# Attention's matmuls as 64x64 tiles, four at a time, in a two-layer convolution kernel

## The chip, the cores and the metric

One core of a Trainium2 chip runs the whole program. The metric is device time in microseconds (us), the median of several runs. PE is TensorE, PEld its weight loads, DVE VectorE, ACT ScalarE, POOL GpSimd, SP SyncE, which here issues nearly all DMAs. PSUM is the memory that PE writes; it is used here in banks of 512 columns of 32 bits.

## What is computed

Two blocks over 8 images of 512 channels and 1024 pixels (tokens), all in 32-bit floats. The first is group norm, q, k, v, attention with 8 heads of 64 channels, a projection, a group norm and the residual. The second is attention with one head of 512 channels over weight-normed projections. Only the first block's attention is touched by the change. Cut to what matters:

```python
hn = group_norm(x, gn1_scale, gn1_bias)
qkv = jnp.einsum('bchw,oc->bohw', hn, w_qkv) + b_qkv[None, :, None, None]
qkv = qkv.reshape(b * NHEAD, 3 * ch, n)
q, k, v = jnp.split(qkv, 3, axis=1)
wgt = jnp.einsum('bct,bcs->bts', q * scale, k * scale)
wgt = jax.nn.softmax(wgt, axis=-1)
a = jnp.einsum('bts,bcs->bct', wgt, v).reshape(b, c, h, w)
out = jnp.einsum('bchw,oc->bohw', a, w_proj) + b_proj[None, :, None, None]
x = x + group_norm(out, gn2_scale, gn2_bias)
# then the second block, on x
```

## The kernel before

**Tiles on PE.** Each 32-bit matmul appears as two records, each with its own weight load; each record streams all columns of the moving operand. A label such as 64\*128 gives the rows and columns of PE's array that a matmul takes: 128\*128 is all of it, 64\*128 one half of the rows (two such matmuls can run side by side on `halves[0]` and `halves[1]`, each into a bank of its own), and 128\*64 one half of the columns (two side by side, into the two halves of one bank's partitions).

**The steps.** An image's attention is 32 steps (`STEPS`, line 370): four pairs of heads `j`, eight blocks `r` of 128 tokens each. `Heads.step` (line 636) issues, for step `i`:

- `softmax(i)`: on DVE two reductions (`nm<-s`, one per head), on ACT two exponentials (`p<-s,nm`).
- in every second step from step 5 on (`LAG`, line 370) `values(g)` (line 611): 16 matmuls of 256 columns into one bank, then one evacuation on ACT (`a<-po`), which frees the slot of `pT`.
- `fill`: in the steps between, one piece of the next pair's q and k. In images 1 to 7 it also holds the last products of the layer before: a 128\*128 one in step 0, and `products_rows` (line 1105, 64\*128) in steps 1 and 2.
- `scores(i + 1)` (line 559): four 64\*128 matmuls of 512 columns into two double banks (tag `sc`, three of them).
- `turn()` (line 586): DVE's transpose (`pb<-p`) of the step before and its four DMAs into `pT`.
- `scale()` (line 604): a reciprocal on DVE, and on POOL two multiplications of `p`.
- `later`: POOL's additions that complete q and k, and other work.

Each engine takes its instructions in the order in which the program issues them (`InOrder`, line 26).

**The pieces of q and k.** `project_rows` (line 398) splits each product by rows: two 64\*128 chains into two banks, evacuated by ACT and added by POOL. It serves image 0, and the first pair of the next image. `project_seven` (line 476), for the other three pairs of images 1 to 7, has four pieces: piece 0 is two whole 128\*128 matmuls of 512 columns; pieces 1, 2 and 3 are eight 64\*128 matmuls each. After piece 0, in the steps 8 and 16, a quarter of the next values is done ahead (lines 1299 to 1301). The steps of image 1 and later in which pieces are projected are set at line 1288.

**Banks.** `bank()` (line 114) takes from two PSUM banks in turn (tag `mm`). The pieces of q and k take both, the values one.

Of the kernel before, what the change touches and what calls it, by code (L numbers as in the profile page):

```python
# [10 lines left out]
AF = mybir.ActivationFunctionType  # L11
# [41 lines left out]
def attention_blocks_kernel(  # L53
# [318 lines left out]

    def project_qk(b, j, hn):
# [24 lines left out]
    def project_rows(b, j, hn, spare):  # L398
# [6 lines left out]
        def pieces():  # L405
            for t in (1, 0):
# [3 lines left out]
                for th in range(2):  # L410
                    hs = slice(th * HN, (th + 1) * HN)
                    pms = [bank(f"pqk_{b}_{j}_{t}_{th}_{r}") for r in range(2)]
                    for ci in range(CI):
                        for r in range(2):
                            PE.matmul(
                                pms[r],
                                w[halves[r], ci, :],
                                hn[halves[r], ci, hs],
                                start=(ci == 0),
                                stop=(ci == CI - 1),  # L420
                            )
# [54 lines left out]
    def project_seven(b, j, right):  # L476
# [13 lines left out]
        def add(to, a, b_):  # L490
            return lambda: PO.tensor_add(to, a, b_)

        adds = (
            ([], []),
            ([], []),
            ([add(q2, q2, q1), add(k2, k2, turned(q2))], [add(k1, k1, k2), add(k2, k2, turned(tmp[1]))]),
            ([add(q1, q1, tmp[0]), add(q2, q2, tmp[1])], [add(q2, q2, tmp[2])]),
        )

        def pieces():  # L500
            pm = bank(f"pq7_{b}_{j}_0")
            run(matmuls(pm, [(w[:, k, :], right(None, 0, k)) for k in range(2)]))
            AC.copy(tmp[1], pm)
            yield adds[0]
            for n in range(1, 4):
                pms = [bank(f"pq7_{b}_{j}_{n}_{r}") for r in range(2)]
                for k in range(CI):
                    for r in range(2):
                        PE.matmul(pms[r], w[halves[r], CI * n - 2 + k, :], right(r, n, k), start=(k == 0), stop=(k == CI - 1))
                if n == 1:  # L510
                    AC.activation(q1, pms[0], AF.Identity, bias=bqs[:, j : j + 1])
                    AC.copy(k1, turned(pms[1]))
                elif n == 2:
# [39 lines left out]
    class Heads:  # L553
        def __init__(self, b, hn, v, qk):
            self.b, self.hn, self.v, self.a = b, hn, v, None
            self.qk = {0: qk}
            self.pT, self.ps, self.waiting, self.open = {}, None, None, None

        def scores(self, i):
# [3 lines left out]
            for c in range(2):  # L563
                cs = slice(c * HN, (c + 1) * HN)
                for hh in range(2):
                    PE.matmul(
                        self.ps[hh][:, cs],
                        qk[halves[hh], 0, r * P : (r + 1) * P],
                        qk[halves[hh], 1, cs],
                        start=True,  # L570
# [924 lines left out]
```

## Time and profile before

| | |
|---|---|
| runs, median of 3 | 3202.4 us (3199.84 to 3202.9) |
| profiled execution, span from first to last instruction | 3197.2 us |
| scores (`s<-qk`), records x mean | 2048 x 603 ns |
| values (`po<-pT,v`), records x mean | 4096 x 382 ns |
| q and k of `project_seven` (`pq`, 64\*128) | 1008 records, mean 589 ns |
| piece 0 of `project_seven` (`pq`, 128\*128) | 84 records, mean 610 ns |
| q and k of `project_rows` (`pqk`, 64\*128) | 640 records, mean 590 ns |
| granted TensorE clock, mean | 0.998 |

The page of the profile gives each engine's busy time, and the chain of work that ended last, followed back from the last instruction. A timeline lists instructions in order of time: start in us, how long, the engine, what it writes and reads (out<-in), the rows\*columns of the array and the shape, how many records were merged (x8), and in brackets how long the engine was idle before it and what ended that. Records of matmuls overlap: a record of 512 columns lasts some 590 ns while the next starts 429 ns after it.

### The profile page before, as it was taken

The page shows a single profiled execution, that of the slowest core. Times are in us where ns is not written, and L with a number is a line of the kernel's source. Part 1 is how long each engine was busy: PE and PEld are TensorE (multiplying, and loading weights), DVE is VectorE, ACT ScalarE, POOL GpSimd, SP SyncE. Part 2 cuts the span into 40 slices and gives each one's busy share as a digit, 9 for nine tenths or more (in the row PEclk, how much of TensorE's full clock was granted, in tenths as well). Part 3 has the DMA queues.
Part 4 walks back from the last instruction along what each step waited for, and adds up shares of the span by engine and source line. Part 5 has one row for each costly group of instructions (what it writes and reads, how often), then busy time and mean ns, then how long its engine had stood idle before and what let it go on. Part 6 is the DMA issues. An engine that isn't in the chain of part 4 may idle for free.

```text
span 3197.2 us, 36929 instructions
## 1 busy us (share of the span) xinstructions
PE 3172.7 (99%) x13374; PEld 1639.4 (51%) x13374; DVE 2286.3 (72%) x3175; ACT 1044.1 (33%) x1810; POOL 1269.7 (40%) x1033
## 2 busy tenths in 40 slices
PE   9999999999999999999999999999999999999899
PEld 5455644556444554445544555445554456444454
DVE  5697767866678766886658866687666877578753
ACT  2453124521145211551215512254023531245310
POOL 1554225732267212761226603366224642246121
PEclk9999999999999999999999999999999999999999
DMA  6777225862268511884128832388224872158600
GB/s 204 209 204 221 76 56 156 220 199 60 56 179 234 178 40 60 210 229 146 48 82 220 225 116 46 112 217 230 93 56 118 218 225 76 30 152 215 191 7 33
DMA packets 225853, 451.59 MB, mean 141 GB/s; under 512 B 21604, under 2 KB 62344, under 8 KB 219912
## 3 DMA queue, kind: packets, MB, share of 16 engines
q1 hardware_dynamic: 225552, 449.20, 50.1%
q8 instruction: 107, 1.75, 0.2%
q14 instruction: 74, 0.61, 0.1%
q10 hardware_dynamic: 120, 0.02, 0.0%
HBM read 137.26 MB, written 29.56 MB: 52 GB/s over the span
## 4 chain that ended last, share of the span: by engine, by line
PE 95%; DMA 2%; DVE 1%; SPq 1%; POOL 1%; issue 0%; ACT 0%; DVEq 0%; POOLq 0%
PE po L34 27%; PE s L34 14%; PE pq L34 7%; PE p_e_T L34 7%; PE p_v_T L34 6%; PE p_e_B L34 5%; PE p_v_B L34 5%; PE pqk L34 5%; PE py L34 4%; PE p_u_T L34 3%; PE p_o_T L34 3%; PE p_u_B L34 3%; PE p_o_B L34 2%; DMA pT<-pb 1%; PE pv L34 1%; PE pG L34 1%
## 5 line engine op out<-in xcount | busy, mean ns | idle before, releaser
L34 POOL TENSOR_SCALAR p<-p,tt 128x1024 f32<-128x1024 f32 x512 | 567.6, 1122 | 728.1 <-DVE tt L34 718.5
L34 ACT ACTIVATE p<-s,nm 128x1024 f32<-128x1024 f32 x512 | 566.2, 1111 | 821.8 <-DVE nm L34 498.4
L34 DVE TENSOR_REDUCE nm<-s 128x1 f32<-128x1024 f32 x512 | 602.5, 1218 | 147.3 <-PE s L34 146.5
L34 DVE STREAM_TRANSPOSE pb<-p 128x2048 f32<-128x2048 f32 x256 | 589.9, 2304 | 39.5 <-DMA pT<-pb 21.6
L34 PE MATMUL s<-qk 64*128 64x512 f32 x2048 | 501.9, 603 | 0.2
L34 PE MATMUL po<-pT,v 128*64 128x256 f32 x4096 | 473.4, 382 | 2.7 <-DMA pT<-pb 2.6
L34 PE MATMUL po<-e,v 128*128 128x512 f32 (+2 forms) x1264 | 449.5, 588 | 0.0
L34 PEld LDWEIGHTS po<-pT,v 128*64 128x64 f32 x4096 | 283.7, 137 | 228.4 <-issue 27.3
L34 PEld LDWEIGHTS po<-e,v 128*128 128x128 f32 (+1 forms) x1264 | 196.3, 189 | 233.9 <-issue 233.1
L34 PEld LDWEIGHTS s<-qk 64*128 64x128 f32 x2048 | 191.6, 186 | 235.5 <-issue 216.7
L34 PE MATMUL pq<-hn,qk 64*128 64x512 f32 (+1 forms) x420 | 191.8, 593 | 0.0
L34 POOL TENSOR_TENSOR esum<-esum,e 128x512 f32<-128x512 f32 x96 | 130.5, 1361 | 154.3 <-ACT e L34 151.8
L34 POOL TENSOR_TENSOR x<-x,o 128x1024 f32<-128x1024 f32 x21 | 52.2, 2514 | 348.9 <-ACT o L34 348.9
L34 POOL TENSOR_TENSOR u<-u,xy 128x512 f32<-128x512 f32 x64 | 79.2, 1270 | 278.6 <-DMA xy<-far_rinv 274.1
L34 ACT ACTIVATE e<-e,shift,rinv 128x512 f32<-128x512 f32 x128 | 101.1, 814 | 256.5 <-DVE e L34 256.5
L34 DVE TENSOR_TENSOR e<-e,p_e_T 128x512 f32<-128x512 f32 x160 | 107.0, 685 | 86.4 <-PE p_e_T L34 84.2
L34 DVE TENSOR_TENSOR v<-v,p_v_T 128x256 f32<-128x256 f32 x300 | 114.4, 419 | 68.9 <-PE p_v_T L34 49.9
L34 PE MATMUL pqk<-hn,qk 64*128 64x512 f32 (+1 forms) x672 | 158.2, 590 | 0.0
L34 PE MATMUL pq<-v,qk 64*128 64x512 f32 x336 | 150.9, 589 | 0.0
L34 PE MATMUL pq<-t,qk 64*128 64x512 f32 x336 | 150.9, 589 | 0.0
L34 PE MATMUL p_e_T<-s,t 128*128 128x512 f32 x320 | 147.8, 592 | 0.0
L34 PE MATMUL py<-x,gram 128*128 128x512 f32 x320 | 141.6, 602 | 4.4 <-DVE x L34 4.4
(224 smaller groups left out, 4116.5 us busy)
## 6 DMA issues: line engine op xcount, KB each, us to landing
pT<-pb SPq DMA_DIRECT2D x1024, 256.0 KB, 4.5
qk<-far_qk SPq DMA_DIRECT2D x21, 896.0 KB
hn<-in_x_dram SPq DMA_DIRECT2D x32, 512.0 KB, 4.5
x<-in_x_dram SPq DMA_DIRECT2D x32, 512.0 KB, 3.7
out_dram<-x SPq DMA_DIRECT2D x31, 512.0 KB, 3.1
score<-far_score SPq DMA_DIRECT2D x8, 1792.0 KB
value<-far_value SPq DMA_DIRECT2D x8, 1792.0 KB
proj<-far_proj SPq DMA_DIRECT2D x7, 1792.0 KB
```

Source lines behind the costliest of these rows:

```text
L34: return lambda *args, **kw: self._pin(call(*args, **kw))
```

## The change

Scores, values, and both ways of projecting q and k become 64\*64 matmuls: each half of the rows is split once more by output columns, and four such matmuls are issued after each other, one for each quarter of the array (`quads`). The values now write two banks, one for each half of the contracted tokens; ACT evacuates the first into `a` and copies the second into a part of `pT` that has been read, and POOL adds them; the slot of `pT` is given back after that. Piece 0 of `project_seven` is gone as a piece of its own: pieces 0 and 1 are done together, for 256 tokens and then for the other 256, with four evacuations each and a POOL addition in place of the row half that a whole matmul summed. The quarter of values done ahead is gone. `products_rows` of the layer before stays as it was.

```diff
--- before.py
+++ after.py
@@ -370,6 +370,12 @@
     STEPS, LAG = CI * NB, 5
     halves = (slice(0, D), slice(D, P))
 
+    def quads(outs, left, right, first=True, last=True):
+
+        for out_, l, r in zip(outs, left, right):
+            for cs in halves:
+                PE.matmul(out_[cs], l[:, cs], r, start=first, stop=last)
+
     def project_qk(b, j, hn):
 
         qk = pair.tile([P, 2, N], F32, tag="qk", name=f"qk_{b}_{j}")
@@ -411,14 +417,7 @@
                     hs = slice(th * HN, (th + 1) * HN)
                     pms = [bank(f"pqk_{b}_{j}_{t}_{th}_{r}") for r in range(2)]
                     for ci in range(CI):
-                        for r in range(2):
-                            PE.matmul(
-                                pms[r],
-                                w[halves[r], ci, :],
-                                hn[halves[r], ci, hs],
-                                start=(ci == 0),
-                                stop=(ci == CI - 1),
-                            )
+                        quads(pms, [w[rs, ci, :] for rs in halves], [hn[rs, ci, hs] for rs in halves], ci == 0, ci == CI - 1)
                     to, rest = qk[:, 0, hs], spare[:, hs]
                     if t:
 
@@ -490,27 +489,38 @@
         def add(to, a, b_):
             return lambda: PO.tensor_add(to, a, b_)
 
-        adds = (
-            ([], []),
-            ([], []),
-            ([add(q2, q2, q1), add(k2, k2, turned(q2))], [add(k1, k1, k2), add(k2, k2, turned(tmp[1]))]),
-            ([add(q1, q1, tmp[0]), add(q2, q2, tmp[1])], [add(q2, q2, tmp[2])]),
-        )
+        adds = {
+            2: ([add(q2, q2, q1), add(k2, k2, turned(q2))], [add(k1, k1, k2), add(k2, k2, turned(tmp[1]))]),
+            3: ([add(q1, q1, tmp[0]), add(q2, q2, tmp[1])], [add(q2, q2, tmp[2])]),
+        }
 
         def pieces():
-            pm = bank(f"pq7_{b}_{j}_0")
-            run(matmuls(pm, [(w[:, k, :], right(None, 0, k)) for k in range(2)]))
-            AC.copy(tmp[1], pm)
-            yield adds[0]
-            for n in range(1, 4):
+
+            def product(pms, n, cols, to):
+                count = CI if n else 2
+                for k in range(count):
+                    quads(
+                        [pm[:, to] for pm in pms],
+                        [w[rs, max(CI * n - 2, 0) + k, :] for rs in halves],
+                        [(right(r, n, k) if n else right(None, 0, k)[rs])[:, cols] for r, rs in enumerate(halves)],
+                        k == 0,
+                        k == count - 1,
+                    )
+
+            low, high = slice(0, TG), slice(TG, HN)
+            for n, cols in enumerate((low, high)):
                 pms = [bank(f"pq7_{b}_{j}_{n}_{r}") for r in range(2)]
-                for k in range(CI):
-                    for r in range(2):
-                        PE.matmul(pms[r], w[halves[r], CI * n - 2 + k, :], right(r, n, k), start=(k == 0), stop=(k == CI - 1))
-                if n == 1:
-                    AC.activation(q1, pms[0], AF.Identity, bias=bqs[:, j : j + 1])
-                    AC.copy(k1, turned(pms[1]))
-                elif n == 2:
+                product(pms, 1, cols, low)
+                product(pms, 0, cols, high)
+                AC.activation(q1[:, cols], pms[0][:, low], AF.Identity, bias=bqs[:, j : j + 1])
+                AC.copy(tmp[1][:, cols], pms[0][:, high])
+                AC.copy(k1[:, :, n * D : (n + 1) * D], turned(pms[1][:, low]))
+                AC.copy(tmp[0][:, cols], pms[1][:, high])
+                yield [add(tmp[1][:, cols], tmp[1][:, cols], tmp[0][:, cols])], []
+            for n in range(2, 4):
+                pms = [bank(f"pq7_{b}_{j}_{n}_{r}") for r in range(2)]
+                product(pms, n, slice(0, HN), slice(0, HN))
+                if n == 2:
 
                     AC.copy(q2, pms[0])
                     AC.activation(k2, turned(pms[1]), AF.Identity, bias=bkq[:, j : j + 1])
@@ -554,7 +564,7 @@
         def __init__(self, b, hn, v, qk):
             self.b, self.hn, self.v, self.a = b, hn, v, None
             self.qk = {0: qk}
-            self.pT, self.ps, self.waiting, self.open = {}, None, None, None
+            self.pT, self.ps, self.waiting = {}, None, None
 
         def scores(self, i):
             j, r = divmod(i, NB)
@@ -562,14 +572,11 @@
             self.ps = [ps_s.tile([P, N], F32, tag="sc", name=f"s0_{self.b}_{i}_{hh}") for hh in range(2)]
             for c in range(2):
                 cs = slice(c * HN, (c + 1) * HN)
-                for hh in range(2):
-                    PE.matmul(
-                        self.ps[hh][:, cs],
-                        qk[halves[hh], 0, r * P : (r + 1) * P],
-                        qk[halves[hh], 1, cs],
-                        start=True,
-                        stop=True,
-                    )
+                quads(
+                    [ps[:, cs] for ps in self.ps],
+                    [qk[rs, 0, r * P : (r + 1) * P] for rs in halves],
+                    [qk[rs, 1, cs] for rs in halves],
+                )
 
         def softmax(self, i):
             p = prob.tile([P, 4, 2, N // 4], F32, tag="p", name=f"p0_{self.b}_{i}")
@@ -608,28 +615,24 @@
                 PO.tensor_scalar(p[:, :, hh, :], p[:, :, hh, :], tot[:, hh : hh + 1], 1.0, ALU.mult, ALU.mult)
             self.waiting = (i, p)
 
-        def values(self, g, most=NT):
+        def values(self, g):
 
             j, t0 = g // (NB // RG), g % (NB // RG) * TG
-            po, s0 = self.open or (bank(f"po0_{self.b}_{g}", TG), 0)
-            s1 = min(s0 + most, NT)
-            self.open = (po, s1) if s1 < NT else None
+            pos = [bank(f"po0_{self.b}_{g}_{r}", TG) for r in range(2)]
             if self.a is None:
                 self.a = big(f"a_{self.b}")
-            for s in range(s0, s1):
-                for hh in range(2):
-                    ch = (2 * j + hh) * D
-                    PE.matmul(
-                        po[halves[hh], :],
-                        self.v[:, s, ch : ch + D],
-                        self.pT[g][:, :, :, hh, s, :],
-                        start=(s == 0),
-                        stop=(s == NT - 1),
-                    )
-            if self.open:
-                return
-
-            AC.activation(self.a[:, j, t0 : t0 + TG], po, AF.Identity, bias=col(BV, j))
+            pT = self.pT[g]
+            for s in range(NT):
+                for po, rs in zip(pos, halves):
+                    for hh in range(2):
+                        ch = (2 * j + hh) * D
+                        PE.matmul(
+                            po[halves[hh], :], self.v[rs, s, ch : ch + D], pT[rs, :, :, hh, s, :], start=(s == 0), stop=(s == NT - 1)
+                        )
+            a, rest = self.a[:, j, t0 : t0 + TG], pT[:, 0, 0, 0].rearrange("p B j -> p (B j)")
+            AC.activation(a, pos[0], AF.Identity, bias=col(BV, j))
+            AC.copy(rest, pos[1])
+            PO.tensor_add(a, a, rest)
             slots.give(f"pT_{self.b}_{g}")
             del self.pT[g]
 
@@ -1296,9 +1299,6 @@
             early, later = [], []
             if i < CI:
                 fill, later = fills[i] + fill, laters[i]
-            if b and r == 0 and 0 < j < CI - 1:
-
-                fill.append(lambda: heads.values((i + 1 - LAG) // RG, 2))
             if r == 0:
                 if j + 1 < CI:
                     heads.qk[j + 1], todo = project_seven(b, j + 1, one.next.right) if b else project_rows(
```

## The prediction

> **What bounds the kernel now.** I read the page's busy table and chain first, then the timeline of one ordinary pair of steps in attention, then the groups of instructions split by shape.
>
> ```profile
> span 3197.2 us, 36929 instructions
> ...
> PE 3172.7 (99%) x13374; PEld 1639.4 (51%) x13374; DVE 2286.3 (72%) x3175; ACT 1044.1 (33%) x1810; POOL 1269.7 (40%) x1033
> ...
> PE 95%; DMA 2%; DVE 1%; SPq 1%; POOL 1%; issue 0%; ACT 0%; DVEq 0%; POOLq 0%
> ```
>
> PE sets the end: 95% of the chain. A busy PE hides gaps here, because a record is drawn longer (589 ns) than the distance to the next one, so only distances between starts count.
>
> ```profile
> 1002.78 0.59 PE L34 MATMUL pq<-v,qk 64*128 64x512 f32 x1
> ...
> 1002.97 2.36 DVE L34 TENSOR_REDUCE nm<-s 128x1 f32<-128x1024 f32 x2 [0.90 <-PE s L34]
> 1003.21 0.59 PE L34 MATMUL pq<-v,qk 64*128 64x512 f32 x1
> ...
> 1004.29 1.11 ACT L34 ACTIVATE p<-s,nm 128x1024 f32<-128x1024 f32 x1 [2.75 <-DVE nm L34]
> ...
> 1005.25 2.30 DVE L34 STREAM_TRANSPOSE pb<-p 128x2048 f32<-128x2048 f32 x1
> ...
> 1005.40 1.11 ACT L34 ACTIVATE p<-s,nm 128x1024 f32<-128x1024 f32 x1
> ...
> 1006.21 1.88 PE L34 MATMUL s<-qk 64*128 64x512 f32 x8
> ...
> 1006.49 1.07 ACT L34 COPY v<-pq 128x512 f32<-128x512 f32 x2
> ...
> 1007.69 2.22 POOL L34 TENSOR_SCALAR p<-p,tt 128x1024 f32<-128x1024 f32 x2 [0.44 <-DVE tt L34]
> 1008.02 3.22 PEld L34 LDWEIGHTS po<-pT,v 128*64 128x64 f32 x32 [0.76 <-ACT v L34]
> 1008.02 3.67 PE L34 MATMUL po<-pT,v 128*64 128x256 f32 x32
> ...
> 1011.63 0.30 PEld L34 LDWEIGHTS s<-qk 64*128 64x128 f32 x4 [0.39 <-issue]
> ...
> 1012.16 0.19 PEld L34 LDWEIGHTS s<-qk 64*128 64x128 f32 x2 [0.24 <-issue]
> ```
>
> Two tiles run side by side, so I count rounds. A round over 512 columns starts 0.429 us after the one before (1002.78, 1003.21), whether two 64x128 tiles or one 128x128; over 256 columns, 0.216 (single records of the values block start at 1008.291, 1008.507, 1008.723; the 128x128 products of 256 columns have 0.216 too). Scores are 4 rounds, so the values should start at 1006.21 + 1.716 = 1007.93; they start at 1008.02, their first weights are loaded only then, and the first round costs 0.267. **Entering the values costs 0.097 + 0.051 = 0.148 us.** Leaving: 16 rounds and 0.051 end at 1011.53, scores start at 1011.63, and their second round comes 0.533 later instead of 0.429. **Leaving costs 0.100 + 0.104 = 0.204.** Between scores and q, k, both 64x128, nothing is lost. So a pair of steps lasts 10.672 us (q, k start at 1002.78 and at 1013.45), and its rounds need 16 x 0.429 + 16 x 0.216 = 10.32.
>
> ```profile
> L34 ACT ACTIVATE a<-po,cols 128x256 f32<-128x256 f32 x128 | 60.8, 475 | 148.8 <-PE po L34 148.5
> ...
> L34 ACT COPY v<-pq 128x512 f32<-128x512 f32 x63 | 34.8, 591 | 36.2 <-PE pq L34 36.2
> ...
> L34 ACT COPY v<-p_v_B 128x256 f32<-128x256 f32 x60 | 20.6, 369 | 231.4 <-PE p_v_B L34 231.4
> ```
>
> These price the evacuations of 256 columns. Per step DVE is busy 2.36 + 2.30 + 0.12 = 4.78 us, 9.56 a pair: it doesn't bind at 10.32.
>
> **The change, part by part.**
>
> *Switches removed.* One shape in attention means no drain, and the next weights load ahead. Each image visits the values 14 times inside its 32 steps; the last visit still goes to 128x128 work, and in image 0 two are entered from a 128x128 product. Saved: 110 entries x 0.148 + 104 exits x 0.204 = 16.3 + 21.2 = 37.5 us. In images 1 to 7 the steps 8 and 16 also hold the 128x128 piece and a quarter of the values: that pair lasts 9.505 us (scores at 970.11, scores at 979.61) and its rounds need 12 x 0.429 + 16 x 0.216 = 8.60, an excess of 0.90, of which 0.352 is counted. 14 x 0.55 = 7.7. **Together -45.2.**
>
> *The rounds themselves.* Four 64x64 tiles stream as many columns as two half tiles: 0.429 and 0.216 kept, +0. No row has four tiles at once. From below nothing can be gained, since columns set the time. From above: eight records a round instead of four; the densest lasting stretches have 0.216 / 4 = 54 ns a record, and at that pace a 256-column round would take 0.432. I take +0 because two tiles cost what one does, to the nanosecond, and because after a true stall (671.37, a DMA awaited) six records of two tiles start within 91 ns, some 15 ns each, against the 27 needed. A page speaks against it. The Trainium skill, "TensorE: Matmul & The Clock Gate", in Part 1 under "Wait — 56ns, not 53.3ns?", says that without hardware decode the sequencer spends about 62 ns on each matmul. By that a round of four would be 0.248, and the sum would be an estimated 80 us higher.
>
> *Piece 0 moved into piece 1's two halves.* Per project_seven 24 rounds of 0.216 for 12 of 0.429: +0.036 x 21 = **+0.8**. No DMA moves.
>
> *New switches.* products_rows stays 64x128, between scores that are now 64x64: two visits an image, 14 x 0.352 = **+4.9**. Step 0 (128x128 layer-1 product, piece, scores) trades one switch for another: 0.
>
> *Four evacuations behind a shorter piece.* After scores end (T0), DVE reduces twice, ACT exponentiates twice, and only then evacuates q and k: in ordinary pairs this starts at T0 + 3.71 (1002.78 to 1006.49) and ends near T0 + 4.87. Values used to need one free bank; they now need both. Ordinary pieces: values are due at T0 + 3.43 + 1.72 = 5.15, a margin of some 0.22 after the semaphore: 0, and the price is in the first rival. For the new halves values are due at 2.59 + 1.72 = 4.31, but ACT has four evacuations of 256 columns. Consecutive ones start some 0.12 us before the last ends (the two copies: 1.07 for 2 x 0.59), so 0.35 + 0.25 + 0.25 + 0.37 = 1.22, until T0 + 4.93. With the semaphore and a first load in the open, PE stands 0.7 us. This happens after both halves for j = 1 and 2 (28 times) and once in step 3 (7; there the next piece waits). Step 0 is covered: a 6.9 us product lies between its scores and the piece. 35 x 0.7 = **+24.5**. Bounds: nothing if it were wholly covered; 1.1 each (four undivided durations, 0.475 + 3 x 0.369), 38. So these pairs take 10.2, and DVE's 9.56 fits.
>
> *Values' second bank.* One copy (0.37) on ACT, behind the exponentials; the banks are free at T1 + 4.5, and the next piece needs them at T1 + 5.17: covered by scores, by 0.6. Then a POOL add of 256 columns, half of an add of 512 (1.28 to 1.36): 0.67. It stands in POOL's queue ahead of the scale of the same step. There POOL reaches it when its other adds end; scale ends 0.6 to 1.2 us later, and the transpose that follows starts after the two reductions, with 0.3 to 0.9 to spare and 0.38 of DVE idle a step behind that: **+1** in all. The slot of pT comes free 1.7 us later, 10 us before it is taken again: 0. After the last image's loop two products wait for `a` (0.56 idle at 3007.79): 2 x 1.05 = **+2.1**. In other images p_o_B, 3.4 us, covers it.
>
> *Image 0's statistics* add two DVE instructions a pair, idle falls to 0.31 a pair, floor 10.36: 4 x 0.04 = **+0.2**.
>
> Sum: -45.2 + 0.8 + 4.9 + 24.5 + 1 + 2.1 + 0.2 = -11.7; span 3185.5. The runs' median, 3202.4, lies 5.2 above the profiled span of 3197.2, so **3191**. Own range: with the stall at 0.5 to 1.1 each, 3184 to 3206.
>
> **The rivals.**
>
> *Slower: POOL's new add delays the softmax.* Scale late, transpose late, reductions late, exponentials late, evacuations late, and now PE waits for both banks. For it: POOL's adds end at 1002.09, 0.08 before scale starts. Against: the margins above; of 89 ordinary pieces only 6 had late reductions. With evacuations 0.5 us later throughout: 78 ordinary pieces x 0.28 + 35 x 0.5 = 39 us more, **3230**. From 0.25 us on the gain is gone.
>
> *Slower by far: four tiles don't keep the pace of two.* There are 128 x 16 + 21 x 24 = 2552 rounds of 256 columns. At 54 ns a record they double: 551 us, **3742**; 5 ns more per round already take the whole gain. Against: the 15 ns above.
>
> *It doesn't do what it says:* the drain goes but first weights still come late, because values wait for ACT. Then 214 x 0.1 = 21 us are saved instead of the main part, **3215**. Against: q, k wait for banks in the same way and lose nothing after scores.
>
> *Faster: the stall is covered* (exponentials earlier, since scores come without their late second round): **3166**.
>
> **How the numbers follow.** Chances: forecast 0.44, stall covered 0.12, late softmax 0.22, late weights 0.07, pace 0.15. A measurement of this kernel tells about 0.2%, 6.4 us, from no change: below 3196 is faster, above 3209 slower. The forecast's 0.44 splits into 0.31, 0.11 and 0.02; of the three slower cases' 0.44, 0.02 falls under each of the first two. Faster: 0.12 + 0.31 + 0.02 = 0.45. Same: 0.11 + 0.02 = 0.13. Slower: 0.02 + 0.40 = 0.42. The range of 8 in 10 runs from the covered stall to a late softmax somewhat beyond its price, 3166 to 3240; outside lie the pace and a little below. The forecast's own range stands above.
>
> **What would show it.** Scores and values in quads of 64*64 records at 0.429 and 0.216 a round; values starting 1.716 after scores; ordinary pairs of 10.32; in steps 8 to 11 values that wait about 0.7 for ACT; new 0.35 around products_rows. Rounds above 0.216, ordinary pairs above 10.5, or idle PE in front of ordinary values would make it wrong.

## The result, and the profile after

The kernel after the change takes 3222.7 us (median of 4 runs, 3217.73 to 3226.55); the kernel before took 3202.65 us beside it. The ratio is 1.0064, 95% interval 1.005 to 1.0079: **slower by some 20 us**, where the forecast was faster by 12. The profiled execution took 3224.0 us, its span is 3222.3 us, 25.1 us more than the span before.

The page of the kernel after, busy times, chain of waits, and the groups that answer to those shown of before:

```profile
span 3222.3 us, 56075 instructions
...
PE 3175.2 (99%) x22426; PEld 1740.2 (54%) x22426; DVE 2280.9 (71%) x3175; ACT 1091.2 (34%) x2043; POOL 1391.0 (43%) x1203
...
PE 69%; POOL 10%; DMA 7%; DVE 6%; issue 4%; SPq 3%; ACT 1%; DVEq 0%; POOLq 0%; ACTq 0%
...
L34 PE MATMUL s<-qk 64*64 64x512 f32 x4096 | 556.7, 592 | 9.0 <-POOL qk L34 6.9
L34 PE MATMUL po<-pT,v 64*64 64x256 f32 x8192 | 511.0, 381 | 11.6 <-DVE mean L34 4.0
...
L34 POOL TENSOR_TENSOR a<-a,pT 128x256 f32<-128x256 f32 x128 | 93.5, 731 | 190.7 <-ACT pT L34 189.4
```

PE's busy share is 99% as before and tells nothing. The chain does: PE's part of it fell from 95% to 69%, and POOL, DMA and DVE now hold a quarter of it. The scores wait for POOL's `qk`, a wait that PE's list of before does not have.

That the four tiles themselves do what they should is seen in an ordinary pair of steps of the kernel after (timeline, PE, image 0):

```profile
143.26 3.75 PE L34 MATMUL pqk<-hn,qk 64*64 64x512 f32 x32
146.69 2.03 PE L34 MATMUL s<-qk 64*64 64x512 f32 x16
148.41 3.77 PE L34 MATMUL po<-pT,v 64*64 64x256 f32 x64
151.86 2.03 PE L34 MATMUL s<-qk 64*64 64x512 f32 x16
153.58 3.75 PE L34 MATMUL pqk<-hn,qk 64*64 64x512 f32 x32
```

From piece to piece it is 10.32 us (143.26 to 153.58), the predicted floor, against 10.672 before. Scores take 1.72 (146.69 to 148.41), the values 3.45 (148.41 to 151.86), so a round of 256 columns in four tiles is still 0.216 us and the switches are gone.

So the loss is elsewhere. This table, worked out from the traces, splits the span by stage; a step is the distance between the starts of DVE's first reductions of two steps, since DVE follows the scores.

| us | predicted change | before | after | change |
|---|---|---|---|---|
| image 0, whole | -4.2 | 385.5 | 398.4 | +12.9 |
| images 1 to 7: steps 0 to 7 | +5.2 | 380.5 | 392.1 | +11.6 |
| steps 8 to 15 | -3.2 | 294.8 | 299.3 | +4.5 |
| steps 16 to 23 | -3.2 | 290.7 | 289.9 | -0.8 |
| steps 24 to 30 | -7.4 | 261.7 | 255.0 | -6.7 |
| step 31 and behind the loop | +1.1 | 1480.4 | 1484.3 | +3.9 |

The rest, -0.3, lies ahead of the first scores. Only the steps 24 to 30 do what the prediction says (in two undisturbed images 37.17 became 36.11, three pairs of 0.35).

**Where image 0 loses.** PE around the group norm of the next image, before:

```profile
189.80 1.88 PE L34 MATMUL s<-qk 64*128 64x512 f32 x8
191.61 0.39 PE L34 MATMUL pm<-mv,gavg 128*128 128x4 f32 x2
192.04 3.67 PE L34 MATMUL po<-pT,v 128*64 128x256 f32 x32
195.64 1.99 PE L34 MATMUL s<-qk 64*128 64x512 f32 x8
```

and after:

```profile
188.08 2.30 PE L34 MATMUL s<-qk 64*64 64x512 f32 x16
190.37 0.36 PE L34 MATMUL pm<-mv,gavg 128*128 128x4 f32 x2
190.81 0.65 PE L34 MATMUL po<-pT,v 64*64 64x256 f32 x4
195.47 6.08 PE L34 MATMUL po<-pT,v 64*64 64x256 f32 x58 [4.00 <-DVE mean L34]
...
208.56 0.39 PE L34 MATMUL pv<-d,gavg 128*128 128x4 f32 x2
208.87 0.65 PE L34 MATMUL po<-pT,v 64*64 64x256 f32 x4
212.93 5.88 PE L34 MATMUL po<-pT,v 64*64 64x256 f32 x58 [3.41 <-DVE ve L34]
```

The small product `pm` takes one of the two `mm` banks. Before, the values used the other one and went on. Now four records of the values run in the free bank and PE stands 4.00 us for the other, until DVE has read `pm`; the same again behind `pv`. DVE is not slow, it is in order (timeline, DVE, after):

```profile
190.17 2.33 DVE L34 TENSOR_REDUCE nm<-s 128x1 f32<-128x1024 f32 x2
192.59 2.31 DVE L34 STREAM_TRANSPOSE pb<-p 128x2048 f32<-128x2048 f32 x1
194.82 0.12 DVE L34 TENSOR_TENSOR d<-mv,pm 128x4 f32<-128x4 f32 x1
...
195.25 0.15 DVE L34 COPY mean<-pm 128x4 f32<-128x4 f32 x1
```

The reading of `pm` is issued in the next step, behind two reductions and a transpose.

The two waits cost more than their own 7.4 us. Within each of them PE's granted clock falls to 0.50, and it stays there for 6.83 us (from 193.99 and from 211.06; it is 1.00 from 186 to 190 and from 201 to 203). Until it is back, the rounds of the values start 0.427 us apart instead of 0.216, so that the 58 records take 6.08 and 5.88 us instead of some 3.46: about 5 us more in the two steps.

**Where images 1 to 7 lose.** POOL ahead of step 16 of image 2, after:

```profile
975.64 1.55 POOL L34 TENSOR_TENSOR qk<-qk 128x512 f32<-128x512 f32 x1
977.17 0.72 POOL L34 TENSOR_TENSOR a<-a,pT 128x256 f32<-128x256 f32 x1
977.87 2.20 POOL L34 TENSOR_SCALAR p<-p,tt 128x1024 f32<-128x1024 f32 x2
980.05 1.26 POOL L34 TENSOR_TENSOR qk<-qk 128x512 f32<-128x512 f32 x1
981.39 1.55 POOL L34 TENSOR_TENSOR qk<-qk,v 128x512 f32<-128x512 f32 x1
982.91 2.21 POOL L34 TENSOR_SCALAR p<-p,tt 128x1024 f32<-128x1024 f32 x2
985.09 2.51 POOL L34 TENSOR_TENSOR qk<-qk,v 128x512 f32<-128x512 f32 x2
```

and what PE's weight loads waited for there:

```profile
986.41 0.21 PEld L34 LDWEIGHTS s<-qk 64*64 64x64 f32 x8 [1.06 <-POOL qk L34]
```

POOL has no gap in these 12 us, and the values' new addition (0.72, at 977.17) stands in the middle. The first of the two additions that start at 985.09 completes q for the next pair of heads, and scores 16 wait for it. The same place before:

```profile
968.77 2.51 POOL L34 TENSOR_TENSOR qk<-qk,v 128x512 f32<-128x512 f32 x2
```

The first of these two ended at about 970.03 and the scores started at 970.11, with their first weights released by it after 0.52 us of idle time, where an ordinary pair has 0.39. So it was just in time, with nothing to spare. PE's weight loads for scores waited for POOL's `qk` 3 times before, 1.3 us in all, and 21 times after, 14.6 us.

A late scale also makes the transposes late. The group of transposes with what its idle time waited for, before:

```profile
L34 DVE STREAM_TRANSPOSE pb<-p 128x2048 f32<-128x2048 f32 x256 | 589.9, 2304 | 39.5 <-DMA pT<-pb 21.6 <-POOL p L34 14.1 <-POOL hn L34 1.2
```

and after:

```profile
L34 DVE STREAM_TRANSPOSE pb<-p 128x2048 f32<-128x2048 f32 x256 | 590.8, 2308 | 86.9 <-POOL p L34 43.3 <-DMA pT<-pb 34.2 <-DVE nm L34 1.7
```

Measured between the starts of scores, and summed over images 1 to 7, the steps 7, 15 and 23, which end in scores of a new pair of heads, are 1.9, 7.2 and 2.8 us longer than before, 11.9 in all; undisturbed each of the 21 would be 0.25 shorter.

### The profile page after: what moved, and what is told of

It is laid out like the page before. It is cut to its first block, busy times and chain, and to the rows that moved or that the text cites. A ratio compares the mean times of both kernels' runs of the same rounds, so it can differ in the third digit from the quotient of the medians.

```text
span 3222.3 us, 56075 instructions
## 1 busy us (share of the span) xinstructions
PE 3175.2 (99%) x22426; PEld 1740.2 (54%) x22426; DVE 2280.9 (71%) x3175; ACT 1091.2 (34%) x2043; POOL 1391.0 (43%) x1203
## 4 chain that ended last, share of the span: by engine, by line
PE 69%; POOL 10%; DMA 7%; DVE 6%; issue 4%; SPq 3%; ACT 1%; DVEq 0%; POOLq 0%; ACTq 0%
PE po L34 18%; PE p_e_T L34 7%; DMA pT<-pb 6%; POOL p L34 6%; PE s L34 6%; PE p_e_B L34 5%; PE p_v_T L34 5%; PE p_v_B L34 4%; PE py L34 4%; DVE pb L34 4%; PE pq L34 4%; PE p_u_T L34 3%; PE p_o_T L34 3%; PE p_u_B L34 3%; SPq L34 3%
## 5 line engine op out<-in xcount | busy, mean ns | idle before, releaser
L34 PE MATMUL s<-qk 64*64 64x512 f32 x4096 | 556.7, 592 | 9.0 <-POOL qk L34 6.9
L34 PE MATMUL po<-pT,v 64*64 64x256 f32 x8192 | 511.0, 381 | 11.6 <-DVE mean L34 4.0
L34 PEld LDWEIGHTS po<-pT,v 64*64 64x64 f32 x8192 | 363.3, 134 | 164.9 <-ACT v L34 28.7
L34 PEld LDWEIGHTS s<-qk 64*64 64x64 f32 x4096 | 207.4, 133 | 222.2 <-issue 151.4
L34 PE MATMUL pq<-hn,qk 64*64 64x256 f32 (+1 forms) x1680 | 202.3, 419 | 0.0
L34 POOL TENSOR_TENSOR a<-a,pT 128x256 f32<-128x256 f32 x128 | 93.5, 731 | 190.7 <-ACT pT L34 189.4
L34 PE MATMUL pqk<-hn,qk 64*64 64x512 f32 (+1 forms) x1312 | 164.1, 589 | 0.0
L34 PE MATMUL pq<-t,qk 64*64 64x256 f32 (+1 forms) x1008 | 156.2, 449 | 1.4 <-DVE v L34 1.4
L34 PE MATMUL pq<-v,qk 64*64 64x512 f32 x672 | 151.6, 590 | 0.0
```

Source lines behind the costliest of these rows:

```text
L34: return lambda *args, **kw: self._pin(call(*args, **kw))
```

## The experiments

Each kernel is the one after the change with one edit. The span is that of one profiled execution; stages not touched differ by 1 to 3 us between such executions.

| run | median, us | ratio to before, interval | span | image 0 | steps 0-7 | 8-15 | 16-23 | 24-30 | behind |
|---|---|---|---|---|---|---|---|---|---|
| after | 3222.7 | 1.0064 (1.005-1.0079) | 3222.3 | 398.4 | 392.1 | 299.3 | 289.9 | 255.0 | 1484.3 |
| statistics read early | 3215.5 | 1.0051 (1.0034-1.0067) | 3214.0 | 385.3 | 391.9 | 299.4 | 290.7 | 256.9 | 1486.9 |
| no POOL add | 3213.7 | 1.0043 (1.0028-1.0058) | 3210.1 | 395.7 | 388.3 | 297.9 | 287.9 | 254.8 | 1482.7 |
| values as before | 3216.6 | 1.005 (1.0035-1.0065) | 3214.6 | 385.2 | 396.2 | 299.8 | 289.4 | 261.9 | 1478.9 |
| add on DVE | 3256.7 | 1.0182 (1.0166-1.0197) | 3263.9 | 401.2 | 392.2 | 298.1 | 291.1 | 255.2 | 1523.7 |
| fetch later | 3228.6 | 1.0082 (1.0063-1.0101) | 3224.3 | 397.0 | 392.0 | 304.9 | 288.5 | 254.3 | 1484.8 |
| no second drain | 3211.9 | 1.0033 (1.0022-1.0045) | 3208.5 | 395.9 | 391.0 | 296.4 | 286.2 | 255.8 | 1479.9 |
| piece 0 as before | 3215.0 | 1.0039 (1.0027-1.0051) | 3212.0 | 398.6 | 383.3 | 299.6 | 287.8 | 255.0 | 1484.3 |
| add at the step's end | 3230.6 | 1.009 (1.0073-1.0107) | 3230.9 | 395.8 | 393.1 | 302.7 | 292.1 | 255.3 | 1488.7 |
| the same, statistics early | 3220.4 | 1.0065 (1.0046-1.0085) | 3217.0 | 386.5 | 392.8 | 300.7 | 290.9 | 255.3 | 1487.8 |
| add held three steps | 3220.4 | 1.0061 (1.0044-1.0078) | 3217.2 | 396.3 | 388.8 | 299.0 | 286.1 | 257.1 | 1486.6 |
| quads late | 3192.3 | 0.9971 (0.9961-0.9981) | 3190.2 | 384.7 | 380.5 | 297.4 | 288.9 | 255.8 | 1479.6 |
| quads late, second form | 3194.2 | 0.9978 (0.9969-0.9987) | 3192.0 | 386.1 | 381.6 | 298.0 | 287.8 | 254.0 | 1482.0 |

The kernel before has 385.5, 380.5, 294.8, 290.7, 261.7 and 1480.4.

### Image 0: the bank of the group norm

```diff
                 if k == 0:
...
                     early += [norm1.aggregate, lambda: next(coeffs)]
+                    later.append(lambda: next(coeffs))
+                elif k == 2:
+                    early.append(lambda: next(coeffs))
+                    later.append(lambda: next(coeffs))
-                elif 0 < k < 8:
+                elif 3 < k < 8:
```

DVE's reading of the two small products now comes in the step that makes them.

> The changed kernel, but in image 0 the group norm's two small products are read from their bank by DVE in the same step in which PE makes them, not one step later. Theory (the values' second bank is what those products still hold, and PE stands until DVE has read them): the two steps that took 7.25 and 6.39 us more than before go back to about 0.2 less than before, some 13 to 14 us in all, less about 1 us for DVE waiting on PE; span near 3210. Rival (the delay of these steps is the statistics' own work on DVE): no more than 2 us.

Image 0 went from 398.4 to 385.3 us, 13.1 less and what it was before the change. PE there, in that run:

```profile
189.26 0.39 PE L34 MATMUL pm<-mv,gavg 128*128 128x4 f32 x2
189.58 0.65 PE L34 MATMUL po<-pT,v 64*64 64x256 f32 x4
191.46 3.46 PE L34 MATMUL po<-pT,v 64*64 64x256 f32 x58 [1.23 <-DVE mean L34]
```

4.00 us of waiting became 1.23, the 58 records behind it take 3.46 us at a granted clock of 1.00, and behind `pv` no wait is left. **Shown:** the stall is the wait for a bank that the group norm held, and the slower clock came with it. The time fell by less (ratio 1.0051 for 1.0064): in the profiled execution the stages behind the statistics gave some of it back.

### The values in one bank

```diff
-            pos = [bank(f"po0_{self.b}_{g}_{r}", TG) for r in range(2)]
+            po = bank(f"po0_{self.b}_{g}", TG)
...
-            for s in range(NT):
-                for po, rs in zip(pos, halves):
-                    for hh in range(2):
...
+            for s in range(NT):
+                for hh in range(2):
+                    PE.matmul(po[halves[hh], :], self.v[:, s, ch : ch + D], self.pT[g][:, :, :, hh, s, :], start=(s == 0), stop=(s == NT - 1))
```

Values as 128\*64, one evacuation, no addition; scores and q, k stay in quads.

> The changed kernel with the values as in the kernel before: two 128x64 tiles, one bank, one evacuation, no POOL addition; scores and q, k stay 64x64, and no quarter is done ahead. Theory: every visit to the values pays 0.352 us of switches again (37.5 us), while image 0's two waits (13 to 14), POOL's lateness (13 to 18) and part of the evacuation waits (5) go: 0 to 8 us above the changed kernel. Rival (the switches are not worth what the rows before say, the quads of the values bring nothing): 25 us or more below the changed kernel.

3216.6 us, 6 less than after, so neither range was met. Image 0 takes 385.2, with no stall, and what lies behind the loop falls by 5.4. But the steps 24 to 30 are back at 261.9 us: with another shape in every second step the switches are there again. The two halves of the change belong together: quads without quads for the values win nothing.

### POOL's addition: left out, with the copy too, on DVE, later

```diff
-            PO.tensor_add(a, a, rest)
```

This leaves out the addition, so the values lack half of the contracted tokens.

> The changed kernel without POOL's addition of the values' second half; so the attention output lacks the contribution of half of the contracted tokens, everything else runs as it was. Theory (the addition delays POOL's q and k additions, and scores at the start of each pair of heads wait for these): steps 15 and 23 of images 1 to 7 lose their 0.3 to 1.8 us of excess, the last image's tail 2 us; together 13 to 18 us less. Rival (ACT's later evacuations alone make PE wait): less than 4 us.

3213.7 us, 9 less, between the two ranges. The steps 7, 15 and 23 together fell from 11.9 us over before to 0.65 (-1.55, +1.97, +0.23), and PE's waits for `qk` ahead of scores from 6.9 us (9 times) to 1.3 (3 times). What this run does not take away: step 12, image 0, the steps 0 to 4.

```diff
-            AC.copy(rest, pos[1])
-            PO.tensor_add(a, a, rest)
```

This leaves out the copy of the second bank as well.

> Leaves out both the ACT copy of values' second bank and POOL's add of it, so the output lacks the second half of the tokens in the values. Theory (the ACT copy was covered, as the prediction says, and only POOL's add costs): 3212 to 3215 us, as the kernel without the add alone (3213.7). Rival (the copy itself makes the next piece wait, in step 12 and behind the loop): 3203 to 3209 us, and step 12 falls by 0.4 us or more.

3211.9 against 3213.7, intervals that overlap: in the loop the copy on ACT was covered, as the prediction had it. Step 12 stayed (5.9 us over before, 6.5 without the addition alone).

```diff
             AC.activation(a, pos[0], AF.Identity, bias=col(BV, j))
-            AC.copy(rest, pos[1])
-            PO.tensor_add(a, a, rest)
...
+            add = lambda: VE.tensor_add(a, a, pos[1])
```

DVE adds the second bank from PSUM at the end of the step's early work (at once behind the loop).

> The changed kernel with the values' second bank added by DVE straight from PSUM, after the step's transpose, in place of ACT's copy and POOL's addition. DVE gets 0.42 us a pair of steps, of which it has 0.7 to spare. Theory (POOL's queue is what is late): 10 to 16 us less, about as without the addition. Rival (any engine's extra drain delays the softmax alike): within 4 us of the changed kernel or slower, with reductions that start late in every second step.

3256.7, far above both ranges. The loss lies behind the loop, +39 us. Two of each image's additions stand there, ahead of DVE's drains of the next layer's products, and DVE, which is in order, stands in front of each until ACT has written `a`: in image 2 6.92 us before the addition at 1085.64 and 3.37 before the one at 1100.52, and PE waits for DVE in turn (1.67 and 2.94 us). The granted clock was 0.50 for 46 us of this run, for 27 after the change. In the loop the steps 7, 15 and 23 are 4.8 us over before instead of 11.9, which fits the theory, but other steps (step 12: 8.0 instead of 4.6) give that back, so this run doesn't settle the matter of POOL.

```diff
-            PO.tensor_add(a, a, rest)
-            slots.give(f"pT_{self.b}_{g}")
-            del self.pT[g]
+            def finish():
+                PO.tensor_add(a, a, rest)
+                slots.give(f"pT_{self.b}_{g}")
+                del self.pT[g]
...
-                self.values((i - LAG) // RG)
+                later = [*later, self.values((i - LAG) // RG, True)]
```

> POOL's add of values' second bank is put at the end of the step on POOL, behind the scale of the softmax and the adds of q, k, instead of in front of them; the slot of pT is given back after it. Nothing is left out. Theory (the add costs by where it stands in POOL's queue: q and k's adds come late and scores 8, 16, 24 wait for them): steps 7, 15 and 23 lose their 0.2 to 2.4 us as they did without the add, time 3211 to 3217 us. Rival (POOL has too little room in steps 12 to 15, wherever the add stands): steps 15 and 23 stay late, 3219 to 3226 us.

Nothing won: the steps 7, 15 and 23 stay late (15.3 us over before, after the change 11.9), as the rival has it, and the time, 3230.6, lies above its range. POOL in that run, image 4, shows why:

```profile
1758.62 1.54 POOL L34 TENSOR_TENSOR qk<-qk,v 128x512 f32<-128x512 f32 x1
1760.12 0.73 POOL L34 TENSOR_TENSOR a<-a,pT 128x256 f32<-128x256 f32 x1
1760.83 2.21 POOL L34 TENSOR_SCALAR p<-p,tt 128x1024 f32<-128x1024 f32 x2
1763.01 2.51 POOL L34 TENSOR_TENSOR qk<-qk,v 128x512 f32<-128x512 f32 x2
```

Moved behind the work of its own step, the addition of step 13 is still ahead of the scale of step 14 and of the last additions for q and k (1763.01), in a run without a gap. So it was held back further:

```diff
+            a, hold = self.a[:, j, t0 : t0 + TG], g % 4 in (0, 1) and g < 12
+            rest = self.a[:, CI - 1, g % 2 * TG :][:, :TG] if hold else pT[:, 0, 0, 0].rearrange("p B j -> p (B j)")
...
-            PO.tensor_add(a, a, rest)
+            if hold:
+                self.held.append((RG * g + LAG + 3, lambda: PO.tensor_add(a, a, rest)))
+            else:
+                PO.tensor_add(a, a, rest)
...
+            if self.held and self.held[0][0] == i:
+                self.held.pop(0)[1]()
```

> POOL's add for the values of the steps 5, 7, 13, 15, 21 and 23 is held back three steps, to the end of the steps 8, 10, 16, 18, 24 and 26, when q and k are complete; ACT copies their second bank into a part of `a` that is written only later, so the slot of pT goes back at once. Nothing is left out. At the end of its own step the add of step 13 still stood in front of the scale of step 14 and of q and k's last adds (1760.12, in an unbroken run of POOL from 1750.01 to 1768.99). Theory (the add costs by being in that unbroken run, and nothing elsewhere): steps 7, 15 and 23 lose the 11 us that they lost without the add, 3212 to 3216 us. Rival (POOL lacks time over the whole of an image's attention, or the cost without the add was the scatter of DMAs): 3219 to 3227 us.

At the place both agree on, the theory holds: the steps 7, 15 and 23 are 2.5 us over before instead of 11.9. The time does not follow: 3220.4, in the rival's range. In the profiled execution the steps 24 to 30 are 2.1 and the part behind the loop 2.3 us longer than after the change. **Shown:** the addition costs where POOL runs without a gap. **Not shown:** that it costs nothing elsewhere; held back, about half of the gain is gone in these two stages, though each differs by no more than untouched stages do.

The addition at the step's end was also combined with the early statistics:

> As the run with the add at the end of the step, and in image 0 the group norm's small products are read by DVE in the step that makes them. If the two causes are independent, the gain in image 0 (13.1 us there) and that of the add's place come together: 3200 to 3207 us, the same as before the change to within its measurement; what is left over before is step 0 to 4 (1.7 us an image), step 12 and what lies behind the loop. Rival (they share their waits): 3210 to 3216 us.

3220.4 against 3230.6: the gain in image 0 (9.3 us in the profile) comes whole, the other does not exist in this form, as the run above shows. Neither range was met; the time lies 4 us above the rival's. The new place of the addition had itself cost 8 us in the run before (3230.6 against 3222.7).

### Step 12: a transfer in front of the transposes

```diff
-            if b and i == NB:
+            if b and i == NB + 2:
                 fetch_qk(CI - 1, b)
```

> The fetch of q and k's next operands (896 KB) is issued at step 10 instead of step 8 in images 1 to 7; all else as after the change. Theory (the fetch holds up the DMAs that carry a transposed block to pT, so that a transpose in step 9 waits for its buffer, and two banks of values are evacuated late in step 12's place): the lateness moves with the fetch; step 12 loses its excess of 0.5 to 1.0 us over the kernel before, a step two later gains it (step 14, an ordinary piece), time 3216 to 3225 us. Rival (step 12 is late because POOL and ACT are, whatever the DMAs do): step 12 keeps +0.5 to +1.0, step 14 stays at -0.1.

All figures here are differences to the kernel before, between the starts of scores, for images 1 to 7. After the change step 12 is +1.06, +0.53, +1.05, +1.06, +0.61, +0.34, -0.03 us; in this run it is -0.1 (one -0.47). Step 14 goes from -0.1 (one +0.31) to +0.13, +1.06, +0.40, +1.06, +1.05, -0.11, -0.11. **The lateness moved by two steps with the transfer.** DVE in image 4, after the change:

```profile
1732.26 2.36 DVE L34 TENSOR_REDUCE nm<-s 128x1 f32<-128x1024 f32 x2 [0.40 <-PE s L34]
1737.05 2.31 DVE L34 STREAM_TRANSPOSE pb<-p 128x2048 f32<-128x2048 f32 x1 [2.43 <-DMA pT<-pb]
```

and with the transfer two steps later:

```profile
1739.75 2.36 DVE L34 TENSOR_REDUCE nm<-s 128x1 f32<-128x1024 f32 x2 [0.55 <-PE s L34]
1745.24 2.31 DVE L34 STREAM_TRANSPOSE pb<-p 128x2048 f32<-128x2048 f32 x1 [3.14 <-DMA pT<-pb]
```

The transpose waits for a buffer that the DMAs into `pT` still read, behind 896 KB. Then the next reductions and exponentials are late, and the scores of step 12 wait for an exponential that frees the bank of their second half. Image 4, after the change:

```profile
1740.64 1.11 ACT L34 ACTIVATE p<-s,nm 128x1024 f32<-128x1024 f32 x1 [3.59 <-POOL p L34]
1741.90 0.21 PEld L34 LDWEIGHTS s<-qk 64*64 64x64 f32 x8 [1.19 <-ACT p L34]
```

In six of the seven images this wait is 0.5 to 1.2 us. The piece of q and k behind it then waits 0.41 us for the evacuation of the values, where 0.28 is usual. Without the second bank's evacuation (the run "no second drain") the wait for the exponential is as long, up to 1.17 us, so that evacuation is not its cause. Before, the transpose waited too (2.12 us in the same place of image 2); PE paid less for it and later, 2.1 us in all in step 13, which after the change is undisturbed in all seven images (5.17 us). Why PE pays more after the change was not separated; it now comes to step 12 out of shorter steps, which may be why.

The time is 6 us above that after the change and above both ranges, though the intervals of the two runs overlap; in the profile the steps 8 to 15 take 304.9 us for 299.3. That step 15, with POOL full, now stands closer behind the transfer may be why; it was not tried.

### The halves of the piece

```diff
+            pm = bank(f"pq7_{b}_{j}_0")
+            run(matmuls(pm, [(w[:, k, :], right(None, 0, k)) for k in range(2)]))
+            AC.copy(tmp[1], pm)
+            yield [], []
...
+            product(pms, 1, every, every)
+            AC.activation(q1, pms[0], AF.Identity, bias=bqs[:, j : j + 1])
+            AC.copy(k1, turned(pms[1]))
+            yield [], []
```

> Pieces 0 and 1 of q and k as before the change (piece 0 as one 128x128 product over 512 columns, piece 1 over 512 columns, now in quads); the rest as after. It takes away the halves with their four evacuations (measured wait about 0.39 us each in steps 9 and 11, 0.33 in step 4) and brings back one visit of 128x128 (about 0.55 us) and an uneven pair of steps: step 8 has only 1.716 + 1.716 us on PE, so DVE's 4.78 us a step binds there. Theory (halves cost about 0.39 a wait): little is won, 3218 to 3230 us. Rival (the wait is the predicted 0.7 us, 35 times): 3200 to 3210 us.

3215.0, 8 us less than after (below the theory's range, above the rival's). The gain is in the steps 0 to 4: +0.63 us over before for each image instead of +1.73. In the steps 8 to 11 of an undisturbed image (and in 16 to 19) the halves were only 0.23 us worse: -0.40 against -0.63. What one half costs there is seen after the change in step 16 of image 2. ACT:

```profile
991.91 0.47 ACT L34 ACTIVATE qk<-pq,bqs 128x256 f32<-128x256 f32 x1
992.27 0.38 ACT L34 COPY v<-pq 128x256 f32<-128x256 f32 x1
992.52 0.40 ACT L34 COPY qk<-pq 128x256 f32<-128x256 f32 x1
992.78 0.41 ACT L34 COPY v<-pq 128x256 f32<-128x256 f32 x1
```

PE's weight loads:

```profile
992.70 0.19 PEld L34 LDWEIGHTS po<-pT,v 64*64 64x64 f32 x4 [0.67 <-ACT v L34]
993.24 3.00 PEld L34 LDWEIGHTS po<-pT,v 64*64 64x64 f32 x58 [0.35 <-ACT v L34]
```

The four evacuations take 1.28 us, as predicted (1.22). But the first two empty the first bank, and four records of the values start then, at 992.70; the others follow when the second bank is free. The scores behind them start at 996.33, where without any wait they would at 990.77 + 1.72 + 3.46 = 995.95: **0.38 us, not 0.70**.

### Quads only where both banks are free

```diff
+    LATE = (24, 16)
...
+                if i < LATE[self.b > 0]:
+                    for hh in range(2):
+                        PE.matmul(self.ps[hh][:, cs], qk[halves[hh], 0, r * P : (r + 1) * P], qk[halves[hh], 1, cs], start=True, stop=True)
+                    continue
...
-                self.values((i - LAG) // RG)
+                (self.values_quads if LATE[self.b > 0] <= i < STEPS - 1 else self.values)((i - LAG) // RG)
...
-                    heads.qk[j + 1], todo = project_seven(b, j + 1, one.next.right) if b else project_rows(
+                    heads.qk[j + 1], todo = (project_seven if (j + 1) * NB > LATE[1] else project_seven_halves_rows)(b, j + 1, one.next.right) if b else project_rows(
```

> Steps 0 to 15 of images 1 to 7 (0 to 23 of image 0), step 31 and everything behind the loop as before the change; scores, values and q, k in quads only from step 16 (24 in image 0) to step 30. Theory (quads win 0.35 us a pair wherever POOL, the two banks and the DMAs leave room, and the losses sit in image 0's statistics, in steps 0 to 15 and behind the loop): steps 24 to 31 1.0 us shorter than before in each image, steps 16 to 24 0 to 0.7 shorter, all else as before: 3190 us (3186 to 3197), faster than before. Rival (the losses come wherever values have two banks): 3200 to 3208 us.

3192.3 us, ratio 0.9971 (0.9961 to 0.9981): **faster than before**, as expected. The page of that run:

```profile
span 3190.2 us, 45020 instructions
...
PE 85%; DMA 5%; DVE 3%; POOL 3%; SPq 2%; issue 1%; ACT 0%; DVEq 0%; POOLq 0%
```

The steps 24 to 30 are 5.9 us shorter than before in images 1 to 7, and image 0 0.9; the steps 16 to 23 win 1.8, with step 23 still 0.04 to 1.26 longer. (Step 17 is 0.02 to 0.66 longer because the halves move work into it; the steps 16 to 19 together win 2.7.) The steps 8 to 15, the same as before but for the last scores, took 2.6 us longer; no run says why. The chain is PE's for 85%, not 95%.

A second form put image 0 in quads too, but for its values in the steps 15 to 21, and POOL's addition at the end of the step:

```diff
-    LATE = (24, 16)
+    LATE = (0, 16)
...
+                if LATE[self.b > 0] <= i < STEPS - 1 and (self.b or not 14 < i < 22):
+                    later = [*later, self.values_quads((i - LAG) // RG, True)]
```

> As the run with quads from step 16 on, with two changes: POOL's add at the end of the step, and image 0 all in quads but for its values in steps 15 to 21, where the group norm's products hold a bank. Theory (each pair in quads wins 0.35 us where both banks are free): image 0 another 2 to 3 us shorter, step 23 by 0.3 us in half of the images: 3188 us (3183 to 3192). Rival (what image 0 wins is lost where its values change shape): 3191 to 3195 us.

Nothing more: 3194.2 (0.9978, 0.9969 to 0.9987), by the rival's range. Image 0 took 386.1 instead of 384.7.

## Why the prediction was wrong

The sum was -11.7 us of span and the measurement +25.1. The saving itself came where nothing disturbed it. The step that failed is what the values' second bank costs others: the prediction put POOL's addition at +1 us in all, and it measured 11; and it put the other users of the two banks at nothing, and the group norm's products in image 0 cost 13.1. That the time came out near the first rival's 3230 is in good part luck: the rival holds neither the bank of image 0 nor scores that wait for `qk`. The terms, as the prediction put them:

- **Switches removed, -45.2: right where nothing else intervenes.** 10.672 became 10.32 in ordinary pairs, 37.17 became 36.11 in the steps 24 to 30. The 0.55 for the 128\*128 piece is in line with the run that has the whole piece: 0.78 of waits at two halves less 0.55 is the 0.23 that it showed. That run has no quarter of the values done ahead, which the 0.55 also held, so the agreement is rough.
- **The rounds, +0: right.** 0.429 and 0.216 held. Four matmul records, one per tile, start in 0.216 us, 54 ns each; the prediction counted their four weight loads too, which makes eight in a round. The rule of the Trainium skill ("TensorE: Matmul & The Clock Gate", Part 1, "Wait — 56ns, not 53.3ns?"), some 62 ns of sequencer for each matmul without hardware decode, did not bind here: by an estimate from it the round would have been 0.248 us.
- **New switches, +4.9: right in kind.** The steps 1 and 2 are 0.97 us longer in each image (0.61 and 0.36), predicted 0.70. "Step 0: 0" left out that a bank is still held there by the last product of the layer before: the halved piece waits about 0.4 us for DVE in all seven images.
- **"Four evacuations behind a shorter piece", +24.5: too dear.** The mechanism was right, the step that failed was "they now need both": only half of the records needs the second bank. 28 visits at 0.38 to 0.41 are 11 us instead of 19.6.
- **"Values' second bank", the slot and the ACT copy: right in the loop. POOL's addition, "+1 in all": the term that failed worst among those that were there.** It measured 11 us in the steps 7, 15 and 23. The margins were read between scale and transpose in an ordinary pair, steps in which POOL has gaps; in the steps 12 to 15 POOL runs without one, and the prediction did not look there. Already before, the scores of a new pair started only 0.08 us behind q's last addition and were released by it. This is the prediction's first rival, in part: transposes waited for POOL 55 times instead of 6. But what PE paid was scores that wait for `qk`, and not every ordinary piece, so its price, 39 us, was too high.
- **Behind the loop** 3.9 instead of 1.1. Three runs without the second bank's evacuation there (values as before, no second drain, quads late) have 1478.9 to 1479.9, as before the change (1480.4), so it comes with that evacuation and its addition; which wait it is was not separated.

And two steps that no term held:

- **A bank is shared with whoever else takes it.** The prediction asked when the q, k pieces leave the banks, and for the next image's statistics priced only DVE's instructions (+0.2). The group norm's products take the same two banks, and DVE reads them only a step later: 13.1 us, shown by the run that reads them early. 7.4 of it are the two waits, about 5 the halved clock behind them.
- **A wait that was there before and mostly covered.** The transpose behind the 896 KB transfer waited 2 us in the trace before as well. There PE paid 2.1 us for it, in step 13; after the change it pays 4.6 in step 12, and 0.7 more of gain not had. That the transfer causes it is shown by moving the transfer; why PE pays more is not shown.

Two small figures of the prediction don't matter here but are off: stalls of 1.1 us each give 3205, not 3206, as the upper end of its own range, and the lines it shows put the end of ordinary evacuations at T0 + 4.78 (1006.49 + 1.07 - 1002.78), not 4.87.

Of the 36.8 us between forecast and result this explains some 29: image 0's banks 13.1; POOL's addition 11.2 less the 1 that was forecast; the rest of the lateness in the steps 7, 15 and 23, which stays without the addition, 5.9 (0.65 over before where 21 x 0.25 = 5.25 less was due); step 12 with its lost gain 5.3, less the 2.1 that step 13 no longer pays; behind the loop 2.8; steps 0 to 4, 1.73 an image instead of 1.44, 2.0; less 8.1 for the cheaper evacuations (28 x 0.29). That the 5.9 come from the additions of the halves, which POOL has to do as well, is argued, not shown. The last 8 us are open; about 4 of them are in image 0, in steps where no single wait stands out, and a stage that a run leaves alone moves by 1 to 3 us.

## What to carry to other kernels

Taking a second accumulator bank makes every user of that pool of banks a partner, so list all of them with the time from allocation to the last reading, also those off the path, before pricing the new shape. Price a small instruction on a side engine in the stage where that engine has no gap, from the addition that arrives just in time there, not by the engine's mean load (40% here). A change that wins 0.35 us a pair and loses several us in a few places is worth applying only to the places where it wins: the two runs that did so were the only ones faster than before.

## What the runs showed of the hardware that was not expected

Four 64\*64 tiles of 32-bit floats keep the pace of two half tiles to the nanosecond that the trace gives, 0.216 us a round of 256 columns, with twice the records. In image 0, within each of two waits of PE, 4.00 and 3.41 us long, the granted clock fell to 0.50 and stayed there for 6.83 us; in a wait of 1.23 us at the same place it stayed at 1.00. With two accumulators that are freed one after the other, PE starts the records whose bank is free (four of 64) and stands at the first one that is not, so a wait is shorter than the last evacuation makes it look. And a few additions of 256 columns an image, put on DVE in front of its drains of the next layer's products, cost 39 us in seven images behind the loop, far more than their own 0.42 us each: DVE stood 6.92 and 3.37 us in front of two of them (image 2), waiting for ACT.
